# The first blocks of a two-layer graph attention kernel: F of one block in two PSUM tiles, and a row block, its dot and index lists requested earlier

## The chip, the cores and the metric

The kernel runs on one core of one Trainium2 chip. The time of a run is the device time of that core in microseconds (us), as a median over runs. In the profile, PE is TensorE (PEld its weight loads), DVE is VectorE, ACT is ScalarE, POOL is GpSimd and SP is SyncE. ACT, DVE, PE and POOL each work through a queue of their own in program order; they wait for one another through semaphores. A profiled execution has a longer span than the timed runs: here 2002.7 us against a median of 1823.62 us. Times of single instructions are on the profile's clock.

## The reference

There are N = 2708 nodes with 1024 features and an adjacency matrix with some 17 neighbours in a row. Two attention layers follow one another, each with a residual and a layer norm.

```python
def layer0(x, adj):
    f = x @ Wf + bf
    g = x @ Wg + bg
    e = relu(f @ g.T)
    a = softmax(where(adj > 0, e, -9e15), axis=1)
    return a @ (x @ W + bW)

def layer1(x, adj):
    h = x @ W1
    e = leaky_relu(h @ a1 + (h @ a2).T, 0.2)
    a = softmax(where(adj > 0, e, -9e15), axis=1)
    return relu(a @ h)

x = layernorm(x + layer0(x, adj))
x = layernorm(x + layer1(x, adj))
```

## The kernel before

The kernel exploits that the matrix is sparse. It has three stages.

**Lists** (0 to about 222 us of the profile). Rows of adj are turned into lists of neighbours, and at the same time PE folds the weights: M stands for Wf times the transpose of Wg, so that the score of a pair is a dot product of a neighbour's row of x with one row of F = x M (plus bias terms). The nodes are sorted by their number of neighbours and cut into 22 blocks: block 0 has 32 rows, the others 128, in four groups of 32 rows each.

**Layer 0** (about 222 to 1190 us), block by block in the order 1, 0, 2, 3, ... 21. A "unit" is one block's work on the neighbours; unit 0 is block 1, unit 1 is block 0, unit 2 is block 2, and so on. One block passes through these steps:

- `load_x(b)`: POOL gathers the block's rows of x into `xb`. This pool has one buffer, so the next block's rows can be loaded only when the last user of these is done. (Block 0's rows go into `zs`.)
- `q_dot(b)` and `q_spread(b)`: a DVE dot of `xb` with the row vector `rb`, and a small PE matmul that spreads the result over partitions; DVE then makes `q[b]`, which the softmax of that unit needs.
- `x_turn(b)`: PE transposes `xb` through PSUM tiles `pt`, ACT copies them to `xT`.
- `f_product(b)`: PE forms F(b) = xT M in a PSUM tile `pm` (two banks, halves h = 0 and 1 of 512 columns; pool `ps_m`, two buffers). Each half takes one bias matmul and eight matmuls, which the profile shows as 16 records.
- `replicate(b, k)`: ACT copies group k's 32 rows of F to all four quarters of a tile `Fr[b, k]`, so that a gathered tile of 128 rows (four neighbours of 32 nodes) meets the right rows.
- `load_lists(b)`: POOL gathers the lists `SL` of the block's groups, one issue for each group. `lay.gathers()` issues the gathers of neighbour tiles into a ring of 20 slots; a slot becomes free when PE has used it in `sums`.
- `dots(u, ...)`: for each neighbour tile one DVE multiply-and-accumulate of 128x1024, about 1.27 us. Unit 0 has 15 tiles, unit 1 has 3, unit 2 has 20. The tiles of a unit are sorted so that those of groups 0 and 1 come first, then those of groups 2 and 3.
- `soft(u)`: softmax over the scores (DVE, with one Exp on ACT), which leaves the weights `st`.
- `lay.sums(u, ...)`: PE adds up the weighted neighbour tiles in the PSUM tile `po`; DVE forms reciprocals `ri` of the sums of the weights; ACT writes `y = po * ri`.
- y is transposed, multiplied by W (`product` with `Wt`), and `close(b)` adds the residual, norms it and writes the result out.

Block 0, with 32 rows, has `f_small`: four partial products side by side in one `pm` tile (`split_product`), an ACT copy of them to `y`, a matmul with the constant `rep` into a second `pm` tile, and an ACT copy to `zs`.

The order of all this is written out by hand. The helper `InOrder` (whose line, L71, nearly every instruction of the profile carries) keeps each engine's instructions in the order of the program, so an instruction that waits holds everything behind it on its engine. A prologue starts blocks 1, 0 and 2; then a loop runs over the units, in which iteration k does the sums of unit k, the products of the block before, x_turn and F of the block two ahead, and the dots and softmax of unit k + 1. In the first iteration (`first`) the steps for the block two ahead are left out, since the prologue or the end of that iteration does them.

Two details matter here. The copies of F(1) into `Fr[1, k]` go half by half, and four of them run on DVE, between copies of the same `pm` tile on ACT. And for block 3 `load_x` is called at the end of iteration 0, so its gather stands on POOL behind the neighbour gathers that iteration 0's sums have set free and behind four lists; `q_dot(3)` opens iteration 1 on DVE.

**Layer 1** (about 1190 us to the end) has the same structure of gathers, sums, a product and a norm, without dots.

Of the kernel before, what the change touches and what calls it, by code (L numbers as in the profile page):

```python
# [8 lines left out]
F32 = mybir.dt.float32  # L9
# [97 lines left out]
def listed_path(ctx, tc, x, adj, Wf, bf, Wg, bg, W, bW, W1, a1, a2, out):  # L107

    nc = tc.nc
    P = 128  # L110
    N, D = x.shape
    KC = D // P
    H = D // 512
    TW = D + 4
    NB = (N + P - 1) // P
# [5 lines left out]
    start = [0] + [valid[0] + P * b for b in range(NB - 1)]  # L121
    groups = [[0]] + [list(range(g, g + 4)) for g in range(1, NG, 4)]
    QT = CAP // 4
    Q = 4
# [8 lines left out]
    pe, dve, act, pool, sp = (InOrder(tc, e) for e in (nc.tensor, nc.vector, nc.scalar, nc.gpsimd, nc.sync))  # L133
# [5 lines left out]
    ps_m = ctx.enter_context(tc.tile_pool(name="ps_m", bufs=2, space=bass.MemoryType.PSUM))  # L139
# [10 lines left out]
    ones3 = const.tile([35, P], BF16, name="ones3")  # L150
# [23 lines left out]
    rows3 = const.tile([35, D], BF16, name="rows3")  # L174
# [5 lines left out]
    def gather(engine, dst, table, idx, rows=N):  # L180
        engine.indirect_dma_start(
            out=dst, out_offset=None, in_=table,
            in_offset=bass.IndirectOffsetOnAxis(ap=idx, axis=0), bounds_check=rows - 1, oob_is_err=False)
# [3 lines left out]
    M = wm.tile([P, KC, D], F32, name="M")  # L187
# [6 lines left out]
    with tc.tile_pool(name="pre", bufs=1) as pre:  # L194
# [54 lines left out]
        with tc.tile_pool(name="adjp", bufs=3) as adjp, tc.tile_pool(name="cands", bufs=2) as cands, \  # L249
# [20 lines left out]
            loaded = []  # L270
# [216 lines left out]
        for b in range(NB):  # L487
            n = nsize[b]
            pe.matmul(pt[:64, 0, :NG], low4[:n, b].rearrange("p j i -> p (j i)"), hot[:n, b, :],
                             start=(b == 0), stop=(b == NB - 1))  # L490
# [42 lines left out]
    def product(n, xT, w, row=None):  # L533


        pm = ps_m.tile([P, H, 512], F32, name="pm")
        for h in range(H):
            c = slice(h * 512, (h + 1) * 512)
            if row is not None:
                pe.matmul(pm[:n, h, :], ones3[row:row + 3, :n], rows3[row:row + 3, c], start=True, stop=False)  # L540
            for k in range(KC):
                pe.matmul(pm[:n, h, :], xT[:, k, :n], w[:, k, c],
                          start=(row is None and k == 0), stop=(k == KC - 1))
        return pm

    def split_product(xT, w, parts, row=None):

        pm = ps_m.tile([P, H, 512], F32, name="pm")  # L550
        for h in range(H):
            c = slice(h * 512, (h + 1) * 512)
            if row is not None:
                pe.matmul(pm[:32, h, :], ones3[row:row + 3, :32], rows3[row:row + 3, c], start=True, stop=False)
            for k in range(KC // Q):
                for p in range(Q):
                    i = p * KC // Q + k
                    pe.matmul(pm[32 * p:32 * p + 32, h, :], xT[:, i, :32], w[:, i, c],
                              start=(k == 0 and (row is None or p > 0)), stop=(k + 1 == KC // Q))
        act.copy(parts, flat(pm))  # L560
        yield
        pm = ps_m.tile([P, H, 512], F32, name="pm")
        for h in range(H):
            pe.matmul(pm[:, h, :], rep, parts[:, h * 512:(h + 1) * 512], start=True, stop=True)
        return pm
# [166 lines left out]
    def load_lists(b):  # L732
        for g in groups[b]:
            gather(pool, SL[:, g, :], LD[:, :], idq[:, g:g + 1], N * Q)
# [9 lines left out]
    with ExitStack() as s0s:  # L744
# [5 lines left out]
        seq = [1, 0, *range(2, NB)]  # L750
        units = cut(R0, 2, seq)
        lay = Layer(units, [ring], D, x, stp)
        xb, q, qd, F, Fr, xTs, yTs, Wp, y, Z = ({} for _ in range(10))

        def load_x(b):
            xb[b] = xp.tile([P, D], F32, name="xb") if b > 0 else zs[:, :D]
            gather(pool, xb[b][:nrows[b]], x, ids[:nrows[b], b:b + 1])

        def dot(a, v, n, col):
            j = jp.tile([P, D], BF16, name="j")  # L760
            dve.scalar_tensor_tensor(j[:n], a, 1.0, v[:n], op0=ALU.mult, op1=ALU.mult, accum_out=col)

        def q_dot(b):
            n = nrows[b]
            qs = small.tile([P, 1], F32, name="qs")
            dot(xb[b][:n], rb, n, qs[:n])
            qd[b] = spread(qs[:n], n, "qd")

        def q_spread(b):
            n = nrows[b]  # L770
            pt = ps_t.tile([P, 4, P], F32, name="pt")
            pe.matmul(pt[:, 0, :Q], rep[:n], qd.pop(b)[:n], start=True, stop=True)
            yield
            q[b] = small.tile([P, Q], F32, name="q")
            dve.tensor_scalar(q[b], pt[:, 0, :Q], s0, None, op0=ALU.add)

        def x_turn(b):
            xTs[b] = tp.tile([P, KC, P], F32, name="xT")
            for _ in turn(xb[b], nrows[b], xTs[b]):
                pass  # L780

        def f_product(b):
            F[b] = product(nrows[b], xTs.pop(b), M, 0)
# [66 lines left out]
        lay.most += len(units[1].tiles)  # L850
        first_gathers(0, 1)
        x_turn(0)
        f_product(1)
        pool.memset(zs[:, D:], 0.0)
        load_lists(3)
        next(spread0)
        for steps in (spread1, spread0):
            for _ in steps:
                pass

        for k in range(Q):
            Fr[1, k] = frp.tile([P, D], F32, name="Fr")
        for h in range(H):
            c = slice(h * 512, (h + 1) * 512)
            for k in range(Q):
                take = dve.tensor_copy if h > 0 and k == 1 else act.copy
                for p in range(Q):
                    take(Fr[1, k][32 * p:32 * p + 32, c], F[1][32 * k:32 * k + 32, h, :])
        f_small()
        x_turn(2)  # L870
        f_product(2)
        act.dma_start(Wt, W.rearrange("(k p) d -> p k d", p=P))
        dots(units[0], 0, len(units[0].tiles))
        lay.most = len(lay.order)
        first_gathers(5, NSL0)
        soft(units[0])
        closing, loaded = iter(()), None
        for k, u in enumerate(units):
            nxt = units[k + 1] if k + 1 < len(units) else None
            b = u.b  # L880
            back = seq[k - 1] if k > 0 else None
            ahead = seq[k + 2] if k + 2 < NB else None

            first = k == 0
            po = ps_s.tile([P, H, 512], F32, name="po")
            y[b] = yp.tile([P, D], F32, name="y")
            if back is not None:
                for _ in yTs[back][1]:
                    pass
            reps = list(range(len(nxt.gs))) if nxt is not None and not first else []  # L890
            for r in reps[:1]:
                replicate(nxt.b, r)
            next(closing, None)
            if loaded is not None:
                q_dot(loaded)
                loaded = None
            next(closing, None)
            for r in reps[1:3]:
                replicate(nxt.b, r)
            lay.sums(u, po, {12: [lambda s=closing: [None for _ in s]]}, y[b])  # L900
            closing = iter(())
            if ahead is not None and not first:
                x_turn(ahead)
            if k + 3 < NB and not first:
                loaded = seq[k + 3]
                load_x(loaded)
            if back is not None:
                load_residual(back)
                if back > 0:
                    Wp[back] = product(P, yTs.pop(back)[0], Wt, 32)  # L910
                else:
                    Wp[back] = whole(split_product(yTs.pop(back)[0], Wt, frp.tile([P, D], F32, name="Fr"), 32))
            spreading = iter(())
            if ahead is not None and not first:
                spreading = q_spread(ahead)
                next(spreading)
            for r in reps[3:]:
                replicate(nxt.b, r)
            if ahead is not None and not first:
                f_product(ahead)  # L920
            if ahead == NB - 1:
                sp.dma_start(M, W1.rearrange("(k p) d -> p k d", p=P))
            yT = tp.tile([P, KC, P], F32, name="xT")
            steps = turn(y[b], nrows[b], yT, halves=True)
            next(steps)
            yTs[b] = yT, steps
            if k + 4 < NB:
                load_lists(seq[k + 4])
            if nxt is not None:
                dots(nxt, 0, len(nxt.tiles))  # L930
            for _ in spreading:
                pass
            if nxt is not None:
                soft(nxt)
            if first:
                q_dot(ahead)
                for _ in q_spread(ahead):
                    pass
                loaded = seq[k + 3]
                load_x(loaded)  # L940
            if back is not None:
                closing = close(back)
                next(closing)
# [11 lines left out]
    with ExitStack() as s1s:  # L955
# [49 lines left out]
        closing = iter(())  # L1005
        waiting = []
        for k, u in enumerate(units):
# [9 lines left out]
            closing = iter(())  # L1017
# [9 lines left out]
            if waiting:  # L1027
                closing = close1(waiting.pop())
# [394 lines left out]
```

## Time and profile before

| what | value |
|---|---|
| time, median of 3 runs | 1823.62 us (1822.46 to 1825.52) |
| profiled span | 2002.7 us |
| PE busy in the span | 1664.6 us (83%) |
| DVE busy | 1174.9 us (59%) |
| ACT busy | 634.7 us (32%) |
| POOL busy | 1191.8 us (60%) |
| mean granted clock of PE | 0.903 |

The shares are averages over stages with different limits; what matters for one stage has to be read from the stretch of the timeline in which it lies. In lines of the timeline the columns are: start (us from the span's start), duration, engine, line, operation, output <- input with partitions x elements, number of merged instructions, and in brackets how long the engine stood idle before it and what ended that. In a list of waits the columns are the total in us, the number of waits and the longest. In a table by stretch each engine has its busy time and, in parentheses, its number of instructions; the last three columns are the granted clock, the busy share of the DMA engines and what they moved.

### The profile page before, as it was taken

To read this page: it belongs to the slowest core of one execution; us is meant where nothing else is said; L and a number is where in the kernel's file an instruction comes from. 1 tells how busy PE (TensorE), PEld (TensorE's weight loads), DVE (VectorE), ACT (ScalarE), POOL (GpSimd) and SP (SyncE) were. 2 spreads that over 40 slices of the span, in tenths; PEclk is the share of its full clock that TensorE was granted. 3 is DMA by queue.
4 is the path that set the end of the run, shared out by engine and by line. 5 is a ranking of instruction groups with operands and counts; after the bars stand their busy time and mean duration, and the time that the engine had idled before them with its cause. 6 is when DMAs were issued, how large, how long until landed. Compare 5 with 4: busy or idle time off the path is not lost. (4 is left out here: it accounts for less than half of the span.)

```text
span 2002.7 us, 22908 instructions
## 1 busy us (share of the span) xinstructions
PE 1664.6 (83%) x7313; PEld 683.8 (34%) x7313; DVE 1174.9 (59%) x3541; ACT 634.7 (32%) x857; POOL 1191.8 (60%) x1191
## 2 busy tenths in 40 slices
PE   5998556899999889999999975468788888887985
PEld 3443222333344333443434432123233333332332
DVE  5879465788888678888888863123232323232332
ACT  4546134444554444445554440011010101011111
POOL 6978445666676456665666531755656565766621
PEclk9999677999999899999999988688889888998988
DMA  6644354656778567876777753887889889998830
GB/s 262 240 170 176 119 220 164 228 199 242 268 285 299 207 226 256 291 258 243 279 277 272 270 215 114 351 298 269 319 300 328 297 306 318 337 330 317 297 145 33
DMA packets 149982, 501.85 MB, mean 251 GB/s; under 512 B 32566, under 2 KB 32598, under 8 KB 147145
## 3 DMA queue, kind: packets, MB, share of 16 engines
q0 software_dynamic: 132032, 427.36, 59.7%
q1 hardware_dynamic: 10202, 55.72, 7.5%
q10 hardware_dynamic: 7618, 17.23, 2.4%
q8 instruction: 59, 0.97, 0.2%
q14 instruction: 71, 0.57, 0.1%
HBM read 509.64 MB, written 33.75 MB: 271 GB/s over the span
## 5 line engine op out<-in xcount | busy, mean ns | idle before, releaser
L71 POOL DMA_INDIRECT ring<-in_x_dram,SL x405 | 437.2, 1079 | 318.6 <-issue 97.0
L71 DVE SCALAR_TENSOR_TENSOR j<-ring,Fr 128x1024 bf16<-128x1024 f32 x402 | 494.8, 1231 | 89.4 <-DMA ring<-in_x_dram,SL 60.2
L71 PE MATMUL pm<-M,yT 128*128 128x512 f32 (+1 forms) x704 | 361.9, 661 | 85.7 <-issue 84.5
L71 POOL DMA_INDIRECT ring<-T,SL x260 | 260.9, 1003 | 166.3 <-issue 58.8
L71 PE MATMUL po<-ring,st 128*32 128x512 f32 x2660 | 346.7, 619 | 6.3 <-issue 6.2
L71 ACT COPY Fr<-pm 32x1024 f32<-32x1024 f32 (+1 forms) x349 | 338.4, 970 | 27.1 <-issue 16.3
L71 PE MATMUL pm<-M,xT 128*128 128x512 f32 (+1 forms) x704 | 316.5, 614 | 16.2 <-issue 15.8
L71 PE MATMUL pm<-Wt,xT 128*128 128x512 f32 (+1 forms) x704 | 309.3, 606 | 1.7 <-issue 1.6
L71 PEld LDWEIGHTS pm<-M,yT 128*128 128x128 f32 (+1 forms) x704 | 138.7, 202 | 301.3 <-issue 300.5
L71 ACT ACTIVATE y<-po,ri 128x512 f32<-128x512 f32 (+1 forms) x88 | 55.9, 684 | 569.3 <-remote 529.3
L71 POOL DMA_INDIRECT more<-T,SL x145 | 145.7, 1005 | 78.4 <-issue 37.8
L71 PEld LDWEIGHTS pm<-M,xT 128*128 128x128 f32 (+1 forms) x704 | 128.6, 191 | 184.2 <-issue 183.6
L71 PEld LDWEIGHTS pm<-Wt,xT 128*128 128x128 f32 (+1 forms) x704 | 126.7, 189 | 157.9 <-issue 157.7
L71 PEld LDWEIGHTS po<-ring,st 128*32 128x32 f32 x2660 | 100.1, 114 | 203.5 <-issue 201.6
L409 POOL TENSOR_TENSOR adj<-adj,iota 128x2708 f32<-128x2708 f32 (+3 forms) x23 | 130.6, 5682 | 28.6 <-ACT adj L71 28.5
L71 DVE TENSOR_TENSOR st<-scores,stack 128x384 f32<-128x384 f32 (+9 forms) x74 | 36.1, 521 | 186.6 <-ACT scores L71 93.0
L71 ACT ACTIVATE scores<-scores 128x24 f32<-128x24 f32 (+5 forms) x44 | 9.6, 219 | 423.0 <-DVE scores L71 253.4
L412 DVE MAX8 cand<-adj 128x8 f32<-128x136 f32 (+2 forms) x440 | 96.6, 284 | 40.3 <-POOL adj L409 40.3
L71 PE MATMUL pm<-halfT,WfT 128*128 128x512 f32 x256 | 113.7, 599 | 0.9 <-ACT WfT L71 0.9
L71 DVE TENSOR_SCALAR scores<-ring,f1q 128x2 f32<-128x2 f32 (+5 forms) x98 | 21.3, 235 | 140.3 <-DMA ring<-T,SL 126.2
L71 POOL DMA_INDIRECT SL<-LD,idq x85 | 87.5, 1030 | 25.8 <-issue 23.9
L71 PE MATMUL po<-more,st 128*32 128x512 f32 x580 | 88.2, 617 | 0.0
(199 smaller groups left out, 1412.3 us busy)
## 6 DMA issues: line engine op xcount, KB each, us to landing
adj<-in_adj_dram SPq DMA_DIRECT2D x21, 1354.0 KB
X1S<-z SPq DMA_DIRECT2D x20, 512.0 KB
ring<-in_x_dram,SL POOLq DMA_INDIRECT x405
u1b<-X1S SPq DMA_DIRECT2D x11, 512.0 KB
rb<-X1S SPq DMA_DIRECT2D x10, 512.0 KB
ring<-T,SL POOLq DMA_INDIRECT x260
rows<-in_L_gnn_Wg_dram ACTq DMA_DIRECT2D x8, 512.0 KB
rows<-in_L_gnn_Wf_dram ACTq DMA_DIRECT2D x8, 512.0 KB
```

Of the source, the lines that this page charges most:

```text
L71: made = self.tc.keep_in_program_order(op(*args, **kwargs))
L409: nc.gpsimd.tensor_tensor(k[:n, cut], k[:n, cut], iota[:n, cut], op=ALU.mult)
L412: nc.vector.max(cand[:n, s, :], k[:n, s * SEG:min((s + 1) * SEG, N)])
```

## The change

The change concerns the prologue of layer 0 and the end of iteration 0.

1. F(1) is made in two `pm` tiles, one for each half (each uses one bank of its tile), so that copies of half 0 can begin while PE still works on half 1. The body of `product` becomes a function `half_product` for that.
2. The copies into `Fr[1, k]` are ordered by pairs of groups, first groups 0 and 1 of both halves, then 2 and 3, and all of them run on ACT.
3. `q_dot(2)` stands on DVE ahead of the dots of unit 0, its spreading matmul on PE behind F(2), and `q[2]` after the softmax of unit 0. Before, all this stood at the end of iteration 0.
4. `load_x(3)` and `load_lists(4)` stand on POOL ahead of the gathers that follow the first dots, and `q_dot(3)` runs in iteration 0 instead of iteration 1.

Nothing is computed that was not computed before; the aim is that first dots, and the work for blocks 2 and 3, can begin earlier.

```diff
         pm = ps_m.tile([P, H, 512], F32, name="pm")
         for h in range(H):
-            c = slice(h * 512, (h + 1) * 512)
-            if row is not None:
-                pe.matmul(pm[:n, h, :], ones3[row:row + 3, :n], rows3[row:row + 3, c], start=True, stop=False)
-            for k in range(KC):
-                pe.matmul(pm[:n, h, :], xT[:, k, :n], w[:, k, c],
-                          start=(row is None and k == 0), stop=(k == KC - 1))
+            half_product(pm, h, n, xT, w, row)
         return pm
...
         x_turn(0)
-        f_product(1)
+
+        halves, xT = [], xTs.pop(1)
+        for h in range(H):
+            halves.append(ps_m.tile([P, H, 512], F32, name="pm"))
+            half_product(halves[h], h, P, xT, M, 0)
         pool.memset(zs[:, D:], 0.0)
         load_lists(3)
...
-        for h in range(H):
-            c = slice(h * 512, (h + 1) * 512)
-            for k in range(Q):
-                take = dve.tensor_copy if h > 0 and k == 1 else act.copy
-                for p in range(Q):
-                    take(Fr[1, k][32 * p:32 * p + 32, c], F[1][32 * k:32 * k + 32, h, :])
+        for ks in ((0, 1), (2, 3)):
+            for h in range(H):
+                c = slice(h * 512, (h + 1) * 512)
+                for k in ks:
+                    for p in range(Q):
+                        act.copy(Fr[1, k][32 * p:32 * p + 32, c], halves[h][32 * k:32 * k + 32, h, :])
+        q_dot(2)
         f_small()
         x_turn(2)
+        load_x(3)
+        load_lists(4)
         f_product(2)
+        spread2 = q_spread(2)
+        next(spread2)
         act.dma_start(Wt, W.rearrange("(k p) d -> p k d", p=P))
         dots(units[0], 0, len(units[0].tiles))
         lay.most = len(lay.order)
         first_gathers(5, NSL0)
         soft(units[0])
-        closing, loaded = iter(()), None
+        for _ in spread2:
+            pass
+        closing, loaded = iter(()), 3
...
-            if k + 4 < NB:
+            if k + 4 < NB and not first:
                 load_lists(seq[k + 4])
...
-            if first:
-                q_dot(ahead)
-                for _ in q_spread(ahead):
-                    pass
-                loaded = seq[k + 3]
-                load_x(loaded)
```

More of the change, by code (lines that the diff above doesn't have):

```diff
@@ L537, in product, with half_product @@
         for h in range(H):
-            c = slice(h * 512, (h + 1) * 512)
-            if row is not None:
-                pe.matmul(pm[:n, h, :], ones3[row:row + 3, :n], rows3[row:row + 3, c], start=True, stop=False)
-            for k in range(KC):
-                pe.matmul(pm[:n, h, :], xT[:, k, :n], w[:, k, c],
-                          start=(row is None and k == 0), stop=(k == KC - 1))
-        return pm
+            half_product(pm, h, n, xT, w, row)
+        return pm
+    def half_product(pm, h, n, xT, w, row=None):
+        c = slice(h * 512, (h + 1) * 512)
+        if row is not None:
+            pe.matmul(pm[:n, h, :], ones3[row:row + 3, :n], rows3[row:row + 3, c], start=True, stop=False)
+        for k in range(KC):
+            pe.matmul(pm[:n, h, :], xT[:, k, :n], w[:, k, c],
+                      start=(row is None and k == 0), stop=(k == KC - 1))
     def split_product(xT, w, parts, row=None):
@@ L862, in listed_path @@
             Fr[1, k] = frp.tile([P, D], F32, name="Fr")
-        for h in range(H):
-            c = slice(h * 512, (h + 1) * 512)
-            for k in range(Q):
-                take = dve.tensor_copy if h > 0 and k == 1 else act.copy
-                for p in range(Q):
-                    take(Fr[1, k][32 * p:32 * p + 32, c], F[1][32 * k:32 * k + 32, h, :])
+        for ks in ((0, 1), (2, 3)):
+            for h in range(H):
+                c = slice(h * 512, (h + 1) * 512)
+                for k in ks:
+                    for p in range(Q):
+                        act.copy(Fr[1, k][32 * p:32 * p + 32, c], halves[h][32 * k:32 * k + 32, h, :])
+        q_dot(2)
         f_small()
         x_turn(2)
+        load_x(3)
+        load_lists(4)
         f_product(2)
+        spread2 = q_spread(2)
+        next(spread2)
         act.dma_start(Wt, W.rearrange("(k p) d -> p k d", p=P))
```

## The prediction

> **What bounds the kernel now.** I first read busy shares and the 40 slices: TensorE is busy 83% of the span and its digit is 8 or 9 nearly everywhere, but slices 5 to 7 (200 to 350 us) show 5, 5 and 6. Then busy time by stretch, cut where the stages change.
>
> ```profile
> core 0: us, PE busy (x) PEld busy (x) DVE busy (x) ACT busy (x) POOL busy (x), PEclk, DMA share, GB/s
> 0.00:222.00 222.00, 171.39 (x605) 83.32 (x605) 172.31 (x850) 109.51 (x154) 162.72 (x118) 0.92 0.52 192
> 222.00:263.00 41.00, 24.89 (x88) 11.05 (x88) 6.49 (x15) 13.37 (x25) 30.77 (x31) 0.75 0.66 234
> 263.00:304.00 41.00, 27.89 (x129) 11.88 (x130) 28.02 (x72) 9.37 (x17) 13.88 (x14) 0.83 0.56 204
> 304.00:357.00 53.00, 37.65 (x95) 15.73 (x94) 32.26 (x69) 19.54 (x24) 23.61 (x23) 0.78 0.41 135
> ...
> 500.00:800.00 300.00, 277.69 (x1186) 114.75 (x1176) 239.24 (x529) 139.68 (x167) 187.72 (x177) 0.95 0.71 256
> ```
>
> From 500 to 800 us PE is busy 277.69 of 300 us: layer 0's steady blocks are bound by PE. From 222 to 357 us it is busy 90 of 135 us and no engine is full: a chain of waits, and the change lies here. The list of waits (222 to 400 us) and the timeline name them.
>
> ```profile
> DVE j L71 <- DMA xb<-in_x_dram,ids: 24.2, 2, 18.4
> PE pt L71 <- DMA xb<-in_x_dram,ids: 20.7, 2, 13.8
> PE pm L71 <- ACT y L71: 19.7, 1, 19.7
> ```
>
> ```profile
> 248.26 11.75 ACT L71 COPY Fr<-pm 32x512 f32<-32x512 f32 x20 [16.33 <-issue]
> ...
> 260.05 2.78 DVE L71 COPY Fr<-pm 32x512 f32<-32x512 f32 x4 [11.25 <-issue]
> ...
> 262.86 4.72 ACT L71 COPY Fr<-pm 32x512 f32<-32x512 f32 x8 [2.85 <-DVE Fr L71]
> ...
> 271.52 1.01 ACT L71 COPY y<-pm 128x1024 f32<-128x1024 f32 x1 [3.94 <-remote]
> ...
> 272.59 3.78 PE L71 MATMUL pm<-y,rep 128*128 128x512 f32 x4 [19.71 <-ACT y L71]
> ```
>
> ```profile
> 320.58 1.00 POOL L71 DMA_INDIRECT xb<-in_x_dram,ids  x1 [0.30 <-issue]
> ...
> 324.75 1.23 DVE L71 SCALAR_TENSOR_TENSOR j<-xb,rb 128x1024 bf16<-128x1024 f32 x1 [18.41 <-DMA xb<-in_x_dram,ids]
> ...
> 324.87 1.08 PE L71 MATMUL pt<-ident,xb 128*128 128x128 f32 x4 [13.78 <-DMA xb<-in_x_dram,ids]
> ...
> 326.43 1.39 ACT L71 ACTIVATE y<-po,ri 32x512 f32<-32x512 f32 x2 [8.61 <-issue]
> ```
>
> Two things to see. Fr of block 1 is copied in one serial chain, 20 ACT, 4 DVE, 8 ACT, from 248.26 to 267.58, and block 0's small product, the transposes of x(2) and F(2) queue behind it. Later, x(3) is issued only at 320.58, after 17 gathers and 4 lists on POOL; DVE stands 18.41 us at the dot with it, with the reciprocal of unit 1 and 20 dots behind, and PE 13.78 us at its transposes. Unit 2's sums start at 359.89; from there PE seldom stops.
>
> [...] DVE's copies begin 0.04 us after ACT's twentieth ends, and ACT resumes as DVE ends. [...] after 19.71 us idle the matmuls with rep took 1061 ns, the same form later 592. [...] here x(3) took 4.2 us from issue to the end of the wait, and I use that.
>
> **The change part by part** (times on the profile's clock).
>
> *Two PSUM tiles, pairs of groups.* PE's matmuls are the same; the half products end at 240.8 and 248.2. A copy costs 11.75 / 20 = 0.588 us. ACT can start half 0 at 240.8: eight copies of groups 0 and 1 to 245.5; half 1 from 248.2 to 252.9; groups 2 and 3 of half 0 to 257.6, of half 1 to 262.3. That is 5.3 us earlier than 267.58, with DVE's four copies (2.78 us) moved to ACT. Groups 0 and 1 are whole at 252.9 instead of 262.8.
>
> *Price of the second tile.* ps_m has two buffers, so block 0's product, which ran at 248.5, now waits for half 0's copies: 257.6. It takes 4.4 us warm; PE will have idled 9 us[...]. I take 7: 264.6. ACT's copy of its parts then starts there. The 3.94 us before that copy in the trace has no releaser that I can name; I take it as gone, and keep +4 for the range. Copy 1.0, rep 3.8 (cold, as now), transposes 1.2: F(2) starts about 271.5 (now 277.3) and ends after 15.1 us at 286.6 (now 292.4).
>
> *q_dot(2) ahead of the first dots.* It waits for x(2), issued at 252.86; DMA traffic drops at 258, so x(2) is in by then. The dot costs 1.3 us, and behind it stand the 15 dots of unit 0, which start at 259.5 instead of 262.86 and end 19.0 us later at 278.5. Softmax (4 us as now) ends at 282.6, before F(2), so this wait costs nothing. q(2) waits for F(2)'s end, since its matmul follows it on PE; nothing behind it is due earlier, as unit 0's sums also follow F(2). They start at 287 (now 292.86).
>
> *x(3) and lists(4) ahead.* x(3) shares one buffer with x(2), so POOL waits for x(2)'s transposes, about 270; lists(3) end at 268.9 and the next gathers wait for the dots (278.5), so nobody is held. x(3) is in at 275. Five POOL issues of 1.3 us leave the stretch 315 to 322. q_dot(3) runs at 287 beside PE's sums; 1.3 us of DVE, hidden, as the sums take 7.07.
>
> *What follows.* Copying now's steps from the sums: their end at 294.1, y(1) at 296.5 (2.3 us later, as now), its transposed copies to 300, the 12 copies of Fr(2) from 300 to 312. Unit 1's sums 299.5 to 304.5; x_turn(3) follows at once, to 306.7 instead of 327.6, with y(0) at 312 instead of 326.4 because the reciprocal no longer stands behind q_dot(3). Block 1's product with W takes 15.8 us (322.5), F(3) 15.0 (338), transposes 0.5: PE could start unit 2's sums at 338.5. On DVE, dots of unit 2 have two groups of Fr at 308; 20 x 1.27 = 25.4 us end at 333, softmax at 337.3. Gathers do not hold them: 18 at 1.3 us from 289 end at 313, plus 4.2 us of landing 317, when the last dots are still 15 us off. So the sums start about 339 instead of 359.9: 21 us. DVE's norm of block 1 then starts level with the sums instead of 3.7 us before them, and ACT's z behind it costs up to 2 us. That leaves 19. The timed median is 9% under the profiled span, and if POOL's issues are slower under the profiler the wait removed is shorter: 22 issues at an assumed 0.05 us less take 1. I predict 18: 1823.6 - 18 = 1805.6.
>
> **The rivals.** (1) F(2) does not come earlier: the unnamed 3.94 us stays and PE is cold, F(2) ends at 292 as now. Then only the x(3) wait goes: 13.8 us on PE, 1810; with 2 to 4 us returned in the next blocks, 1813. For it: PE's idle before block 0's product is new. Against: ACT starts 7.4 us earlier. (2) A new wait eats it all: unit 2's dots meet gathers that have not landed, as unit 3's now do at 368 to 383, and the sums start near 358: 1822, same. Against: POOL issues them 23 us before their dots. (3) Slower: block 0's product behind the copies, then parts, rep, transposes and F(2) all late. With every cost at its upper end F(2) ends at 299, 6.6 us late; if x(3), which now waits for x(2)'s transposes, also brought back its wait, 1830. Against: its 13.8 us leave even in rival 1. (4) Larger: block 0's product stays warm and no DVE level with PE: 23 to 25 us, 1799.
>
> **How the numbers follow.** Forecast (1800 to 1809) 0.64, rival 1 (1809 to 1815) 0.19, rival 4 0.08, rival 2 and what lies between 0.05, rival 3 0.04. Faster 0.92, same 0.04, slower 0.04. The range reaches from rival 4's end to rival 1's late end: 1798 to 1814.
>
> **What would show each step.** After: 32 ACT copies of Fr with no DVE copy, the first at 240.9; first dot of unit 0 near 259.5; block 0's product near 257.6; F(2) ending near 287; no DVE wait on xb over 3 us between 285 and 360; unit 2's sums near 339. Layer 0 after 400 us should be the same blocks, shifted. Wrong: F(2) ending later than 292, dots of unit 2 that wait for ring gathers by several us, or sums of unit 3 (403.7 now) less than 12 us earlier.

## The result, and the profile after

| | before | after |
|---|---|---|
| time, median of 4 runs each, taken side by side | 1823.04 us (1822.0 to 1825.52) | 1801.85 us (1799.45 to 1806.64) |
| ratio to before | | 0.9885, 95% interval 0.9862 to 0.9908 |
| profiled span | 1822.8 us (second trace, below) | 1799.5 us |

The change saves 21.2 us; 18 were forecast (1805.6 us). One thing must be said of conditions. The execution behind the trace of before that is shown ahead of the prediction took 2004.8 us, while the timed ones took 1823. From `after_again` on, every execution of every kernel below takes about 2000 us; these ran on another chip (number 0) than the four runs before them (number 6), and whether it was the chip or the hour is not known. A profiled execution is not longer in general: in `b_again`, a second trace of before, the span is 1822.8 us and the timed median 1828.3. So here `b_again` stands for before, and times are compared only among executions made side by side. Ratios are taken from each kernel's faster executions alone, since the runs of about 2000 us scatter by 45 us and more; medians are of all.

The spans of the two traces differ by 23.3 us. Of these, 3.9 lie ahead of layer 0, in the lists, which the change doesn't touch.

The page's 40 slices of after, now 45 us each, first the busy tenths of PE and further down its granted clock:

```profile
PE   5999279899999999999999997828989889889995
...
PEclk9999679899999999999999998959999999999997
```

The hole that stood at 200 to 350 us has shrunk to one slice, the fifth (180 to 225 us), nearly all of which belongs to the lists, with a 7 behind it. The table by stretch gives it in numbers, first for after:

```profile
222.00:263.00 41.00, 29.08 (x88) 11.78 (x88) 10.89 (x22) 20.80 (x37) 31.22 (x31) 0.69 0.68 240
263.00:304.00 41.00, 39.10 (x177) 16.86 (x178) 29.41 (x78) 17.16 (x24) 25.03 (x25) 1.00 0.74 270
304.00:357.00 53.00, 44.37 (x206) 17.35 (x205) 47.31 (x101) 27.48 (x33) 29.24 (x29) 0.93 0.63 228
...
500.00:800.00 300.00, 288.13 (x1310) 122.58 (x1309) 261.82 (x584) 147.18 (x178) 201.60 (x189) 0.99 0.75 271
```

and for `b_again`:

```profile
222.00:263.00 41.00, 26.12 (x88) 11.49 (x88) 5.43 (x13) 13.21 (x24) 30.81 (x31) 0.75 0.66 234
263.00:304.00 41.00, 31.97 (x148) 13.41 (x148) 30.64 (x77) 14.18 (x23) 15.67 (x15) 0.85 0.62 226
304.00:357.00 53.00, 33.46 (x80) 14.77 (x78) 32.52 (x68) 14.93 (x18) 21.87 (x21) 0.77 0.36 117
...
500.00:800.00 300.00, 290.18 (x1284) 123.40 (x1284) 262.08 (x586) 149.18 (x182) 203.51 (x192) 0.99 0.77 277
```

From 222 to 357 us PE is busy 112.6 us instead of 91.6: 21 us more work inside the same 135 us, some 4 of them because layer 0 begins 3.9 us earlier in this trace. The steady stretch is as before. PE's clock from 263 to 304 us is 1.00, where it was 0.85. The timeline of after, from F(1) to unit 2, answers to the lines shown of before:

```profile
238.09 4.68 ACT L71 COPY Fr<-pm 32x512 f32<-32x512 f32 x8 [10.14 <-PE pm L71]
...
245.48 14.18 ACT L71 COPY Fr<-pm 32x512 f32<-32x512 f32 x24 [2.70 <-PE pm L71]
...
254.96 0.58 PE L71 MATMUL pm<-rows,ones 3*32 3x512 bf16 x1 [9.21 <-ACT Fr L71]
255.33 1.23 DVE L71 SCALAR_TENSOR_TENSOR j<-xb,rb 128x1024 bf16<-128x1024 f32 x1 [9.32 <-DMA xb<-in_x_dram,ids]
...
262.36 1.01 ACT L71 COPY y<-pm 128x1024 f32<-128x1024 f32 x1 [2.71 <-PE pm L71]
...
263.43 1.99 PE L71 MATMUL pm<-y,rep 128*128 128x512 f32 x4 [1.14 <-ACT y L71]
...
266.56 1.46 POOL L71 DMA_INDIRECT xb<-in_x_dram,ids  x1 [0.93 <-PE pt L71]
...
281.81 1.22 DVE L71 SCALAR_TENSOR_TENSOR j<-xb,rb 128x1024 bf16<-128x1024 f32 x1
...
294.00 1.09 PE L71 MATMUL pt<-ident,xb 128*128 128x128 f32 x8
...
303.92 1.38 ACT L71 ACTIVATE y<-po,ri 32x512 f32<-32x512 f32 x2
...
328.52 0.29 PE L71 MATMUL pt<-rs,stack 128*32 128x1 f32 x14 [2.79 <-DVE rs L71]
```

Read it by the brackets. Fr is 32 copies on ACT, none on DVE. Block 0's product waits 9.21 us for ACT, the price of the second PSUM tile. x(3) is issued at 266.56, and POOL stood only 0.93 us for the transposes of x(2). The dot with x(3) at 281.81 and its transposes at 294.00 carry no bracket, where the first trace of before had 18.41 and 13.78 us. The last line opens unit 2's sums. In `b_again` the same places read:

```profile
269.77 3.78 PE L71 MATMUL pm<-y,rep 128*128 128x512 f32 x4 [15.77 <-ACT y L71]
...
318.52 1.00 POOL L71 DMA_INDIRECT xb<-in_x_dram,ids  x1 [0.31 <-issue]
...
322.85 1.23 DVE L71 SCALAR_TENSOR_TENSOR j<-xb,rb 128x1024 bf16<-128x1024 f32 x1 [21.32 <-DMA xb<-in_x_dram,ids]
...
322.96 1.09 PE L71 MATMUL pt<-ident,xb 128*128 128x128 f32 x4 [18.93 <-DMA xb<-in_x_dram,ids]
...
324.52 1.38 ACT L71 ACTIVATE y<-po,ri 32x512 f32<-32x512 f32 x2 [12.16 <-DVE ri L71]
```

ACT's wait in the last line is for a reciprocal that stood on DVE behind the dot with x(3).

### The profile page after: what moved, and what is told of

Same layout as the page of the kernel before. It is cut to its first block, busy times and chain, and to the rows that moved or that the text cites. A ratio compares the mean times of both kernels' runs of the same rounds, so it can differ in the third digit from the quotient of the medians.

```text
span 1799.5 us, 22910 instructions
## 1 busy us (share of the span) xinstructions
PE 1573.3 (87%) x7313; PEld 669.9 (37%) x7313; DVE 1172.8 (65%) x3537; ACT 636.4 (35%) x861; POOL 1187.0 (66%) x1191
## 5 line engine op out<-in xcount | busy, mean ns | idle before, releaser
L71 ACT COPY Fr<-pm 32x1024 f32<-32x1024 f32 (+2 forms) x353 | 340.7, 965 | 21.0 <-PE pm L71 16.3
L71 PE MATMUL po<-ring,st 128*32 128x512 f32 x2660 | 340.6, 619 | 0.1
L71 POOL DMA_INDIRECT ring<-T,SL x260 | 259.4, 998 | 84.9 <-issue 57.2
L71 PE MATMUL pm<-M,xT 128*128 128x512 f32 (+1 forms) x704 | 311.5, 622 | 0.4 <-ACT xT L71 0.4
L71 PE MATMUL pm<-Wt,xT 128*128 128x512 f32 (+1 forms) x704 | 303.5, 599 | 0.0
L71 PE MATMUL pm<-M,yT 128*128 128x512 f32 (+1 forms) x704 | 298.5, 595 | 0.3 <-ACT yT L71 0.3
L71 PEld LDWEIGHTS pm<-M,yT 128*128 128x128 f32 (+1 forms) x704 | 127.2, 186 | 170.2 <-issue 169.7
L71 POOL DMA_INDIRECT more<-T,SL x145 | 144.7, 998 | 44.6 <-issue 32.6
L71 PEld LDWEIGHTS po<-ring,st 128*32 128x32 f32 x2660 | 104.9, 115 | 185.6 <-issue 182.4
L71 PE MATMUL pt<-rs,stack 128*32 128x1 f32 x680 | 13.8, 177 | 118.0 <-DVE rs L71 68.8
L71 POOL DMA_INDIRECT SL<-LD,idq x85 | 86.0, 1012 | 25.8 <-issue 20.9
```

The lines of the kernel that those rows point to most:

```text
L71: made = self.tc.keep_in_program_order(op(*args, **kwargs))
```

## The experiments

To compare traces that start layer 0 at slightly different times, I count from the first matmul of F(1) in each trace. "Ahead" means fewer us from there than in `b_again`.

| start of, us after F(1) | b_again | only_copies | only_ahead | x3_late | after |
|---|---|---|---|---|---|
| F(1) itself, us of the span | 231.34 | 230.31 | 230.14 | 231.54 | 227.46 |
| sums of unit 0 | 58.7 | 52.0 | 57.2 | 52.8 | 54.1 |
| sums of unit 2 | 126.9 | 120.5 | 104.1 | 120.7 | 101.1 |
| sums of unit 4 | 212.7 | 207.0 | 191.6 | 207.9 | 188.8 |
| sums of unit 14 | 633.4 | 627.5 | 612.7 | 631.9 | 611.8 |
| layer 1's first matmul | 966.6 | 960.1 | 944.5 | 964.8 | 945.3 |
| ratio of times to before | 1.0006 | 0.9996 | 0.9897 | 0.997 | 0.9885 |

**`b_again`.** No edit: the kernel before.

> The kernel before once more, unchanged, for a second trace of it. The span of its first trace (2002.7 us) is 9% over its timed median; the one of the changed kernel (1799.5 us) is not. If the excess is an oddity of that one execution, this trace has a span near 1823 us, and the idle times of 3.94 us and 17.0 us before ACT's two copies to y, which had no releaser, are gone or shorter. If it belongs to this kernel under the profiler, the span is near 2000 us again. Either way the dot with x(3) should wait about 18 us. Time: the same as before.

Measured: ratio 1.0006 (0.9991 to 1.0022). Its trace puts unit 2's sums at 126.9 us after F(1), the first trace of before at 128.4. So the first trace had the length of this region right within 1.5 us, and its other 178 us lie elsewhere. Three lengths inside the region differ, and all matter below: PE's wait for x(3) (18.93 here, 13.78 there), unit 1's sums (2.75 against 4.94 us), and the idle before ACT's copy of block 0's parts (none, against the unnamed 3.94).

**`only_copies`.** The two PSUM tiles and the copies by pairs of groups, put into before; nothing else moves.

```diff
-        f_product(1)
+        halves, xT = [], xTs.pop(1)
+        for h in range(H):
+            halves.append(ps_m.tile([P, H, 512], F32, name="pm"))
+            half_product(halves[h], h, P, xT, M, 0)
...
+        for ks in ((0, 1), (2, 3)):
+            for h in range(H):
...
         f_small()
         x_turn(2)
         f_product(2)
```

> Parts 1 and 2 alone (two PSUM tiles for F(1), copies by pairs of groups on ACT); x(3), lists(4), q_dot(2) and q_dot(3) stand where they stood. My theory: F(2) ends about 7 us earlier, so sums of unit 0, the gathers that they set free and x(3) behind these all start 7 us earlier; the 18 us wait of DVE for x(3) stays. Time 5 to 7 us less than before, 1816 to 1818. Rival (the copies carry the whole gain): 18 to 21 us less, 1802 to 1805. Rival (the early copies are hidden behind the wait for x(3)): 0 to 1 us less.

Measured: 1825.01 us over 20 runs, ratio 0.9996 (0.9979 to 1.0013), that is -3.8 to +2.4 us. The trace has unit 2's sums 6.4 us ahead, but the timed runs show none of it: my expectation was wrong. What the trace does show is that the copies don't touch the wait for x(3):

```profile
310.83 1.00 POOL L71 DMA_INDIRECT xb<-in_x_dram,ids  x1 [0.30 <-issue]
315.03 1.23 DVE L71 SCALAR_TENSOR_TENSOR j<-xb,rb 128x1024 bf16<-128x1024 f32 x1 [21.22 <-DMA xb<-in_x_dram,ids]
315.11 0.72 PEld L71 LDWEIGHTS pt<-ident,xb 128*128 128x128 f32 x4 [19.71 <-issue]
315.14 1.09 PE L71 MATMUL pt<-ident,xb 128*128 128x128 f32 x4 [18.83 <-DMA xb<-in_x_dram,ids]
```

Everything ahead of the wait is some 6 us earlier, the issue of x(3) is too, and DVE and PE stand as long as in `b_again` (21.32 and 18.93 us). The span of this one profiled execution is 1817.4 us, and that execution (1819.33 us timed) is among the fastest of the 20; whether the usual execution gives the 6 us back later, its trace can't say.

**`only_ahead`.** The other half alone: q_dot(2), x(3), lists(4) and q_dot(3) early as in after, F(1) in one tile and the old copies. (This edit, and those of the runs below, are shown against after.)

```diff
-        halves, xT = [], xTs.pop(1)
-        for h in range(H):
-            halves.append(ps_m.tile([P, H, 512], F32, name="pm"))
-            half_product(halves[h], h, P, xT, M, 0)
+        f_product(1)
...
-        for ks in ((0, 1), (2, 3)):
+        for h in range(H):
...
+                take = dve.tensor_copy if h > 0 and k == 1 else act.copy
```

> Parts 3 and 4 alone (q_dot(2), x(3), lists(4), q_dot(3) ahead); F(1) in one PSUM tile with its copies as before. My theory: F(2) ends as before, the waits of DVE (18 us) and PE (14 us) for x(3) go, and unit 2's sums start 14 to 18 us earlier: time 14 to 16 us less than before, 1807 to 1809. Rival (the copies carry the gain): at most 3 us less. Rival (the parts need each other, since the copies decide when x(2)'s buffer is free for x(3)): less than 8 us.

Measured: 1807.02 us, ratio 0.9897 (0.9858 to 0.9935), -18.8 us. Unit 2's sums are 22.8 us ahead and layer 1 starts 22.1 us ahead. This half alone is nearly the whole change. (The profiled execution took 1803.9 us, the median of the four is 1807.02.) DVE and PE have no wait for x(3) left; what DVE now meets is ACT's copies of Fr(2):

```profile
299.75 1.09 PE L71 MATMUL pt<-ident,xb 128*128 128x128 f32 x8
301.52 1.23 DVE L71 SCALAR_TENSOR_TENSOR j<-ring,Fr 128x1024 bf16<-128x1024 f32 x1 [3.91 <-ACT Fr L71]
305.59 1.23 DVE L71 SCALAR_TENSOR_TENSOR j<-ring,Fr 128x1024 bf16<-128x1024 f32 x1 [2.84 <-ACT Fr L71]
```

The same two waits, 3.91 and 2.84 us, stand in after, at 295.78 and 299.85.

**`x3_late`.** After, with x(3), lists(4) and q_dot(3) back at their old places; q_dot(2) stays early.

```diff
         x_turn(2)
-        load_x(3)
-        load_lists(4)
         f_product(2)
...
-        closing, loaded = iter(()), 3
+        closing, loaded = iter(()), None
...
-            if k + 4 < NB and not first:
+            if k + 4 < NB:
...
+            if first:
+                loaded = seq[k + 3]
+                load_x(loaded)
```

> The changed kernel with x(3), lists(4) and q_dot(3) back at their old places (end of iteration 0, q_dot(3) in iteration 1); q_dot(2) stays ahead of the first dots. My theory: it falls back to what the copies alone give, 1816 to 1818, and DVE again waits 15 to 18 us for x(3). Rival (q_dot(2) ahead of the dots is what helps, because ACT and PE get q(2) sooner): it stays within 3 us of the changed kernel, 1800 to 1805.

Measured: 1819.05 us over 10 runs, ratio 0.997 (0.9948 to 0.9993), -5.5 us. The wait is back in full, 22.37 us on DVE and 19.30 on PE:

```profile
316.14 1.23 DVE L71 SCALAR_TENSOR_TENSOR j<-xb,rb 128x1024 bf16<-128x1024 f32 x1 [22.37 <-DMA xb<-in_x_dram,ids]
```

Of the 6.2 us by which unit 2's sums are ahead in its trace, 4.8 are left at unit 4 and 1.8 at layer 1. (The profiled execution took 1824.3 us, the median of the ten is 1819.05, so its trace needn't show what most of them lose.) Unit 4 shows one way of losing them. PE's timeline of `x3_late`:

```profile
439.44 0.30 PE L71 MATMUL pt<-rs,stack 128*32 128x1 f32 x15 [3.48 <-ACT xT L71]
...
439.59 10.46 PE L71 MATMUL po<-ring,st 128*32 128x512 f32 x79
```

and of `b_again`:

```profile
443.99 0.29 PE L71 MATMUL pt<-rs,stack 128*32 128x1 f32 x14 [2.41 <-ACT xT L71]
...
444.14 8.76 PE L71 MATMUL po<-ring,st 128*32 128x512 f32 x79
```

The wait for ACT grew from 2.41 to 3.48 us, and the same 79 records of matmuls then took 10.46 instead of 8.76 us: 1 us of wait became 2.8 us. The granted clock tells the same: over 430 to 500 us it is 0.98 in `x3_late` and 1.00 in `b_again`. The length of the wait alone doesn't decide: a wait of 1.88 us (`x3_late`, unit 9), one of 2.02 us (`b_again`, unit 6) and one of 2.08 us (after, unit 11) were followed by sums of 10.5 us too, and one of 2.75 us (after, unit 13) by sums of 8.76 us.

The next eight runs were made under the 2000 us conditions, in two series, in which before has medians of 2019.8 and 2022.2 us. In each series one run is after itself: `after_again` in the first, `after_c` in the second.

**`after_again`, `after_c`** (after, unchanged), **`only_copies2`, `ahead_c`** (the two halves again).

> The changed kernel once more, unchanged, timed beside the others of this call. If its gain is the 14 to 20 us of the wait for x(3) and nothing of the copies' 6 us, the ratio is near that of the second half alone, 0.990 (18 us); if both halves add up, 0.986 (25 us).

> The kernel with the copies' parts alone once more, for a second trace. The first one had unit 2's sums 6.4 us earlier than before and kept 5 to 6 us to its end, but the timed runs show no gain. If later blocks give the 6 us back in most executions, this trace again has the sums of unit 2 at 120.5 us after the start of F(1), and loses several us between there and layer 1. If the first trace was an accident already at unit 2's sums, it has them near 127.

> The changed kernel unchanged, to be timed beside the next three; the call before this one ran under conditions in which every kernel took about 2000 us with a spread of 50 us, and told nothing of differences of a few us. Ratio to before 0.986 to 0.990.

> The second half of the change alone (x(3), lists(4), q_dot(2), q_dot(3) ahead; copies as before), beside the whole change. If the halves add up, it is 5 to 6 us slower than the changed kernel. If the copies' gain is given back by the later blocks, it is within 2 us of it, although its unit 2's sums start 3 us later (104 against 101 us after the start of F(1)).

Measured ratios: `after_again` 0.992 (0.987 to 0.997), `after_c` 0.9876 (0.9739 to 1.0014), `only_copies2` 1.0005 (0.9955 to 1.0054), `ahead_c` 0.9976 (0.9938 to 1.0014). The whole change still gains, by about 16 us in `after_again`; the interval of `after_c`, from three executions, reaches 1. In the trace of `only_copies2` unit 2's sums start 129.6 us after F(1), no earlier than in the first trace of before (128.4). The traces show why the copies give nothing here: ACT's copy of block 0's parts, on which F(2) depends, starts at 268 to 274 us of the span however early ACT is free. In `after_again`:

```profile
246.06 14.18 ACT L71 COPY Fr<-pm 32x512 f32<-32x512 f32 x24 [2.70 <-PE pm L71]
...
268.24 1.01 ACT L71 COPY y<-pm 128x1024 f32<-128x1024 f32 x1 [8.00 <-remote]
```

The copies of Fr end at 260.2 there, then ACT stands 8.00 us. The view names no releaser, but the trace's records of semaphores do: this copy waits for PE's semaphore alone, and that rises at 268.21, 5.3 us after the last recorded matmul of block 0's product ended (262.90). In all nine traces of these conditions, the first of before among them, the signal comes 40.0 to 40.3 us after F(1) starts, whether the product ended 5 or 19 us before it. In the five usual traces it comes less than 0.1 us behind the product. So here block 0's product can be moved without moving what ACT waits for. What holds PE's signal back is open. `ahead_c` has unit 2's sums at 113.3 us after F(1), as early as `after_c` with 112.6, and loses its gain right behind them: unit 3's sums start at 171.7 against 157.3. Why is open too, and since their intervals overlap, the times of the two can't be told apart.

**`lists_late`, `lists_c`.** After, with lists(4) alone back in iteration 0.

```diff
         load_x(3)
-        load_lists(4)
         f_product(2)
...
-            if k + 4 < NB and not first:
+            if k + 4 < NB:
```

> The changed kernel with lists(4) alone back at its old place behind the gathers of iteration 0; x(3) stays ahead. My theory: nobody waits for these lists before unit 4, and POOL has room: within 2 us of the changed kernel, unit 2's sums at the same place. Rival (the four issues stand in front of x(4) and hold the next block): 3 to 5 us slower than the changed kernel.

> The changed kernel with lists(4) alone back at its old place behind the gathers of iteration 0. My theory: hidden, since nobody waits for these lists before unit 4: unit 2's sums at 101 us and the time within 2 us of the changed kernel. Rival (they delay x(4) and the residual behind them): 3 to 5 us slower.

Measured: 0.9972 (0.9927 to 1.0018) beside `after_again`'s 0.992, and 0.9904 (0.9855 to 0.9952) beside `after_c`'s 0.9876. The intervals overlap in both pairs, so the times don't say what the lists are worth; the expectation of 2 us and its rival of 3 to 5 us both stand. Unit 2's sums are 116.6 and 115.9 us after F(1), against 113.2 and 112.6, and 128.4 in the first trace of before. At this place x(3) early with the lists late keeps some 12 of 15 us. The remaining 3 us can't be laid on the lists: the spans of these two traces are also 38 and 23 us longer than those of `after_again` and `after_c`.

**`further`, `further_c`.** An attempt to beat after: half 1 of F(1) in the banks of `po`, so that block 0's product doesn't wait for a `pm` tile, and ACT's copy of its parts put ahead of the last 16 copies of Fr.

```diff
-            halves.append(ps_m.tile([P, H, 512], F32, name="pm"))
+            halves.append(ps_m.tile([P, H, 512], F32, name="pm") if h == 0 else ps_s.tile([P, H, 512], F32, name="po"))
...
+        copies(0, 1)
+        tiny = split_product(xTs.pop(0), M, yp.tile([P, D], F32, name="y"), 0)
...
+        copies(2)
         x_turn(2)
+        copies(3)
+        dots(units[0], 0, 8)
         q_dot(2)
```

(It also sorts unit 0's tiles of groups 2 and 3 by group, and copies two groups of F(2) ahead of unit 0's sums.)

> The changed kernel taken further: half 1 of F(1) in the idle banks of po, block 0's product copied right after the first pair of groups, x(2)'s transposes before the last group's copies, q_dot(2) behind eight dots of unit 0, and two groups of Fr(2) copied before y of block 1. Worked out from the changed kernel's trace, counted from the start of F(1): first dots at 22.5 us (now 29.5), F(2) ends at 47 (now 54), unit 2's sums start at 92 to 94 (now 101). If what is won at unit 2's sums stays won, time 7 to 9 us less than the changed kernel. Rival (later blocks give back what is won in PE's and DVE's first steps, as the copies alone seem to show): at most 3 us less than the changed kernel, although unit 2's sums do start 7 us earlier.

> The version taken further once more: first dots at about 20 us after the start of F(1) (changed kernel 29.5), F(2) ending at 47 (54), unit 2's sums at 92 to 94 (101). If what is won there stays won, 7 to 9 us less than the changed kernel; if later blocks give it back, at most 3 us less.

Measured: 1.0002 (0.9964 to 1.004) and 0.9998 (0.9945 to 1.005): no gain over before, in the series in which after has 0.992 and 0.9876. Unit 2's sums start 117.6 and 117.2 us after F(1), later than in after there (113.2 and 112.6), where 92 to 94 were expected. ACT and DVE in `further`:

```profile
272.22 1.01 ACT L71 COPY y<-pm 128x1024 f32<-128x1024 f32 x1 [19.09 <-remote]
...
282.56 1.23 DVE L71 SCALAR_TENSOR_TENSOR j<-ring,Fr 128x1024 bf16<-128x1024 f32 x1 [18.72 <-ACT Fr L71]
```

The copy stood in front of the other copies of Fr, waited 19.09 us for the same late signal of PE (at 272.19, the product having ended at 253.04), and held them; DVE then stood 18.72 us at the first dot that needs group 2. The plan rested on that copy being free to start, which these conditions don't allow. Whether it beats after under the usual ones was not tried.

## Why the prediction was right, and where its sizes were off

Times of the first trace's clock in the prediction are turned into us after F(1) by taking 231.45 off.

| step, us after F(1) | predicted | after | b_again |
|---|---|---|---|
| copies of Fr(1) end | 30.9 | 32.2 | 37.3 |
| block 0's product starts | 26.2 | 27.5 | 18.3 |
| first dot of unit 0 | 28.1 | 29.5 | 32.6 |
| F(2) ends | 55.2 | 53.9 | 58.7 |
| transposes of x(3) start | 73.1 | 66.5 | 91.6 |
| y(0) | 80.6 | 76.5 | 93.2 |
| F(3) ends | 106.6 | 97.8 | |
| unit 2's sums start | 107.6 | 101.1 | 126.9 |

**Right: the copies and their price.** Copies end 5.1 us earlier; 5.3 were predicted. Everything in the table's first three rows is 1.3 to 1.4 us later than predicted, because the first half of F(1) took 10.05 us where the first trace of before had 8.9; that is not the change's doing, since `b_again` has 10.09. Block 0's product idles 9.21 us (9 taken) and takes 7.3 (7 taken, an estimate from 4.4 warm and from rep, whose matmuls took 1061 ns cold against 592).

**Right: q_dot(2) costs nothing.** It stands 9.32 us, and the 15 dots with it, which could otherwise begin 19.1 us after F(1), as in `only_copies` (249.38 of its span). But in after the softmax is over at 280.3 and F(2) at 281.4, so the wait stays hidden, with 1 us to spare. What the copies by pairs gave DVE has been spent on this dot; what they still give is F(2), 4.8 us earlier.

**Mis-sized: the matmul with rep.** I took 3.8 us, cold. PE was warm: 1.99 us at a granted clock of 1.00, after 1.14 us of idle. In `b_again` it is 3.78 after 15.77. The product that was moved behind the copies now runs directly ahead of rep and warms PE: its first half took 3.64 us, its second 2.72. The idle time has not gone, it has moved to where the product pays for it. PE worked for 6.2 us here before it was warm: the granted clock is 0.50 from the product's start at 254.96 to 261.2 and 1.00 behind that. The warm rep (1.8 us) is one part of what pulled F(2) back from 1.3 us late to 1.3 early. Another is a slip in the prediction's sum: copy, rep and transposes lead from 264.6 to 270.6, and it wrote 271.5.

**Lucky: the unnamed 3.94 us.** The prediction took this idle time as gone without a reason. It is gone under the usual conditions, but the change didn't remove it: `b_again` hasn't got it either, and `after_again` has it.

**Right: the wait for x(3), and mis-sized: what PE stood.** This is the main step. I took 13.8 us of PE from the first trace; the second has 18.93. The wait also cooled PE: the first half of the product with W that follows took 8.99 us in `b_again` and 7.13 in after (the first and the second line here).

```profile
326.24 8.99 PE L71 MATMUL pm<-Wt,xT 128*128 128x512 f32 x16
...
295.34 7.13 PE L71 MATMUL pm<-Wt,xT 128*128 128x512 f32 x16
```

I kept 15.8 us for the whole product, it took 14.7. Two further terms copied from the first trace were longer there than usual: y(1) 2.3 us behind its sums, where PE's signal was late again (the usual traces have 0.1), and unit 1's sums at 5.0 us, which took 2.75. Together they bring F(3) 8.8 us ahead of my forecast. Of that, 2.79 us end in a wait for DVE's rs (the last line of after's timeline): unit 2's sums are 6.5 us ahead of the forecast and the gain there is 25.8 us, not 21.

**Mis-sized: what comes back.** I allowed 3 us: 2 for ACT's z in the blocks behind, and 1 for POOL's issues being slower under the profiler. The second rested on the first trace's long span and has no ground: POOL issues every 1.30 us in both traces of before. Of the first, after shows no added wait between units 2 and 3. The lead is 25.8 us at unit 2's sums, 24.1 at unit 3's, 25.1 at unit 10's, 24.3 at unit 11's, 21.6 at unit 14's and 21.3 at layer 1. So 4.5 us return. The first 1.7 follow from the wait of 2.79 us ahead of unit 2's sums: the clock is 0.50 from 329.5 to 332.9 us, and the sums take 13.03 us where `b_again` has 11.34.

```profile
328.67 13.03 PE L71 MATMUL po<-ring,st 128*32 128x512 f32 x79
```

That the allowance came near is therefore luck in its cause. `b_again` has a slow spell of its own at unit 6, which gives some of it back:

```profile
527.73 0.29 PE L71 MATMUL pt<-rs,stack 128*32 128x1 f32 x14 [2.02 <-ACT xT L71]
...
527.88 10.46 PE L71 MATMUL po<-ring,st 128*32 128x512 f32 x79
```

Most of the rest goes between units 10 and 14. PE's timeline of after at units 11, 12 and 13:

```profile
710.83 0.29 PE L71 MATMUL pt<-rs,stack 128*32 128x1 f32 x14 [2.08 <-ACT xT L71]
...
710.98 10.46 PE L71 MATMUL po<-ring,st 128*32 128x512 f32 x79
...
754.49 0.29 PE L71 MATMUL pt<-rs,stack 128*32 128x1 f32 x14 [1.50 <-DVE rs L71]
...
797.95 0.30 PE L71 MATMUL pt<-rs,stack 128*32 128x1 f32 x15 [2.75 <-DVE rs L71]
```

and the same three in `b_again`:

```profile
739.01 0.29 PE L71 MATMUL pt<-rs,stack 128*32 128x1 f32 x14 [1.28 <-ACT xT L71]
...
739.16 8.76 PE L71 MATMUL po<-ring,st 128*32 128x512 f32 x79
...
781.02 0.29 PE L71 MATMUL pt<-rs,stack 128*32 128x1 f32 x14 [1.28 <-DVE rs L71]
...
822.97 0.29 PE L71 MATMUL pt<-rs,stack 128*32 128x1 f32 x14 [1.23 <-DVE rs L71]
```

PE waits 6.33 us instead of 3.79 there, and the sums behind the first of these waits take 10.46 us instead of 8.76: 2.5 and 1.7 us, together what is lost between units 10 and 13. So PE, busy 288 of 300 us in the steady blocks, still waits for ACT and DVE at some hand-overs, and a wait can cost a slow spell besides. But these are two single executions. Every execution's own jitter is in them, and in `only_ahead` the loss is smaller (22.8 to 22.1). Where the time returns is shown for this pair of traces. The wait ahead of unit 2's sums belongs to the early x(3): it is 2.77 us in `only_ahead` too, and 0.40 us in `b_again`, `only_copies` and `x3_late`. For the waits at units 11 to 13 no such tie is shown.

**The rivals.** Rival 1 (the unnamed 3.94 us stays, F(2) no earlier) fell under the usual conditions, where there is no such wait. Under the others its premise holds: in `after_again` F(2) ends 61.7 us after F(1), in the first trace of before 61.0. Rival 2 (late gathers take x(3)'s place) fell: unit 2's dots wait for ACT's copies of Fr, 3.91 and 2.84 us. Rival 3 (slower) fell: F(2) is early. Rival 4 (more: block 0's product warm, DVE not level with PE) had neither premise right: the product ran at a granted clock of 0.50 for 6.2 of its 7.3 us, and DVE's level with PE remained, as the 2.79 us show. That the gain at unit 2's sums exceeds 25 us all the same comes from the terms above: rep, the transposes, and PE's longer wait.

**How the two halves add.** 18.8 us by parts 3 and 4 alone (q_dot(2), x(3), lists(4), q_dot(3)), 21.2 with the copies. Within these parts x(3) and q_dot(3) were never moved apart, and q_dot(2) never alone. The copies alone are worth 0 (-3.8 to +2.4), and as part of `x3_late`, together with an early q_dot(2), 5.5 us (1.3 to 9.5). Both intervals admit 1.3 to 3.8 us gained, and so does the difference of the first two figures; the runs don't give it more closely.

## What to carry to other kernels

When one buffer serves several blocks in turn, ask at what instant it becomes free and issue the next load there, not where its user stands in the program: in `b_again` the buffer's last user, the dot with x(2), came 24 us after the transposes (275.3 to 299.3) and the next load 18 us after that dot (300.5 to 318.5), and the next dot then held the reciprocal and 20 dots behind it on DVE. Making everything ahead of such a wait earlier moved the wait here without shortening it. When a wait goes, price the clock with it: behind PE's 18.93 us the first half product took 1.9 us longer than without the wait. And take a second trace of before: a single one can come from an execution unlike the timed ones, as here.

## What the runs showed of the hardware

- Under the 2000 us conditions PE's semaphore for block 0's product rose 40.0 to 40.3 us after F(1) started in every kernel, 5.2 to 19.2 us behind the product's last recorded matmul, and ACT's copy (128x1024) waited for it until 268 to 274 us of the span. Under the usual ones it rose 0.04 to 0.06 us behind that matmul.
- A slow spell of PE can follow a short wait, and the wait's length alone doesn't tell: the same sums of a unit took 10.5 us behind waits of 1.88, 2.02, 2.08 and 3.48 us, and 8.8 us behind waits of 2.41 and 2.75 us. In after the granted clock is 0.84 over the 10.46 us at unit 11 and 1.00 over the 8.76 us at unit 12.
- A product that moved warmed its neighbours: in `b_again` PE idled 15.77 us ahead of rep, in after 9.21 us ahead of block 0's product and 1.14 ahead of rep. The product took 7.3 instead of 4.4 us (254.96 to 262.3, and 249.59 to 254.0), rep 1.99 instead of 3.78, and the transposes of x(2) behind it 1.04 instead of 1.92. The cost and the gain are nearly equal, 2.9 and 2.7 us.
